# Softmax weights of a small attention copied by DMA instead of spread by matmuls, in a four-stage convolution kernel

## The chip, the cores and the metric

The kernel runs on one core of a Trainium2 chip. Its engines work side by side, each through its own queue of instructions: TensorE (PE; its weight loads are listed as PEld), VectorE (DVE), ScalarE (ACT), GpSimd (POOL) and SyncE (SP), whose queue only starts transfers here. ACT's queue starts transfers too. The transfers themselves run on 16 DMA engines. The metric is device time in microseconds (us), the median of several runs. Less is better.

## The reference

Four convolution-like stages run one after the other on an array x of 8 images, 16 channels and 128 x 128 points, all in float32. The change touches the first: at every point the 3 x 3 neighbourhood is read as three tokens (one for each column) of 48 numbers, which pass through a transformer block with four heads of 12 numbers each.

```
x = fold(in_x)                                # N x 3 tokens x 48, one N for each point
q, k, v = split(layernorm(x) @ w_attn.T, 3)   # each as 4 heads of 12
att = softmax(q . k / sqrt(12))               # 3 x 3 for each point and head
x = x + (att @ v) @ w_attn_proj.T
x = x + gelu(layernorm(x) @ w_fc.T) @ w_fc_proj.T
out = sum over tokens of layernorm(x), through conv_w, + conv_b
```

The other three stages are a gated chain of 1 x 1 convolutions, a convolution of rational functions and a spline convolution. They need what the stage before them wrote.

## The kernel before

**Tiling.** The first stage works on four image rows at a time, a step; there are 32. A tile has two images in its 128 partitions (g = 0 and 1, partitions 64 g and up) and 512 points in its free dimension; so the eight images make four tiles k, which are worked in two halves d, of two tiles each. The tokens of a point are shifted copies of one another along the row: the windows u = 0, 1, 2 of a padded row. So q, k and v are computed once for each point, and the token u of a point takes its neighbours' k and v.

**Steps in flight.** The loop `for n in range(-2, NCH + 3)` (L688 on) holds up to four steps at once: `ahead` (n + 2: its input rows are loaded and centred), `then` (n + 1: layer norm, q, k, v, scores, softmax), `new` (n: attention, projection, first half of the MLP) and `old` (n - 1: rest of the MLP, last norm), and `done` (n - 2: written out). The body issues all their operations in one hand-written order; PE's are tied to it by `in_turn("pe", ...)`, and so are some of DVE's and POOL's. The list `between` holds eight slots: in each, one piece of the attention (`attend`) is followed by pieces of other work.

**Softmax.** `then.softmax` (L510 on) leaves weights in the tile `att`, 96 partitions x 3 x 512: partition 32 u + 8 k + 4 g + h holds the weights of token u, tile k, image g and head h. Its last instruction is the product with the reciprocal of the sum (L529, DVE).

**Attention.** Since the three weights sum to one, a token's result is a middle v plus weighted differences of neighbouring v (`dv`). `attend(k, j, at)` (L533 on) is called eight times a step. It spreads the weights of the heads over the partitions of their numbers with three matmuls against the 0/1 matrix `spread` (into PSUM, `banks`), multiplies them on DVE with the windows of `dv` (L543), and joins the two parts on POOL (L551 and L553). `project(d, u)` (L556 on) multiplies the result with the projection weights on PE and adds the residual on DVE (L565).

**MLP.** `unit(i)` is the MLP for token and half i = 0 to 5: `normed` (a PE product and `h` on DVE, L638), `hidden` (PE and GELU on ACT, `hid`) and `back` (PE, then the residual on DVE, L662). Units 0 to 3 of a step run at the end of its own turn of the loop, units 4 and 5 in the slots of the next.

**PSUM.** PE's results go into eight banks, handed out in pairs by `two()`; while `attend` runs, `ring["from"]` keeps some of them for it.

**Buffers.** Tiles come from pools with a fixed number of buffers; a tile that finds none free waits for the last reader of the oldest. `work` has 11 buffers of 4 KB for each partition, `large` 5 of 6 KB, `xc` 5 of 4 KB. The 0/1 matrices and small constants lie in one tile, `const`, kept through the whole kernel; the weights of the second stage (`w1s`) are loaded at the start of the first.

Of the kernel before, what the change touches and what calls it, by code (L numbers as in the profile page):

```python
# [36 lines left out]
def _constants():  # L37
# [20 lines left out]
    score[token, 24 + 4 * g + h] = 1.0  # L58
    parts["score"] = score
    spread = np.zeros((128, 4, 128))  # L60
    bcast = np.zeros((128, 5, 128))
    last = np.zeros((128, 2, 2, 32))
    for t in range(4):
        bcast[32 * t + 16 + g, 4, token] = 1.0
        for n in range(4):
            bcast[32 * t + 4 * (n // 2) + 2 * (n % 2) + g, n, token] = 1.0
            spread[32 * t + 8 * n + 4 * g + h, n, token] = 1.0
        for u in range(2):
            for k in range(2):
                last[32 * t + 8 + 4 * u + 2 * k + g, u, k, 16 * g + c] = 1.0  # L70
    parts["spread"] = spread.reshape(128, 512)
# [34 lines left out]
def kernel(  # L106
# [29 lines left out]
    from_ = _WHERE["pair"][1]  # L136
    const = cpool.tile([128, _CONST.shape[1] - from_], F32, name="const")
    nc.scalar.dma_start(const, const_in[:, from_:])

    def k_(name):  # L140
        n, lo, hi = _WHERE[name]
        return const[:n, lo - from_ : hi - from_]
# [83 lines left out]
    w1s, b1s = [], []  # L226
    for n in range(5):
        t = cpool.tile([BC, BC], F32, name=f"w1_{n}")
        nc.gpsimd.memset(t, 0.0)
        for b in range(B):  # L230
            r = slice(b * C, (b + 1) * C)
            loads.append((t[r, r], w1[n].rearrange("i o -> o i") if n < 2 else w1[n]))
        w1s.append(t)
        b1s.append(rep(b1[n], B, f"b1_{n}"))
# [7 lines left out]
    with ExitStack() as l0:  # L242
# [19 lines left out]
        def k0(name):  # L262
# [4 lines left out]
        spread, bcast = (  # L267
            k0(name).rearrange("p (n m) -> p n m", m=128) for name in ("spread", "bcast")
        )
# [27 lines left out]
        for i in range(3):  # L297
            for g in range(2):
                r = slice(64 * g + i * 16, 64 * g + i * 16 + 16)
                nc.scalar.dma_start(  # L300
                    wqkv[r, :, :E], w0_qkv[i].rearrange("c (n o) -> c n o", n=3)
                )
                nc.scalar.dma_start(wfc[r], w0_fc[i])
                nc.scalar.dma_start(wcv[r, g * 16 : (g + 1) * 16], w0_conv[i])
# [11 lines left out]
        for g in range(2):  # L316
            nc.scalar.dma_start(wpc[64 * g : 64 * g + E, :E], w0_proj)
# [39 lines left out]
        def work(name):  # L357
            return tmp.tile([128, 2, 512], F32, tag="work", name=name, bufs=11)

        def large(name):  # L360
            return tmp.tile([128, 3, 512], F32, tag="large", name=name, bufs=5)
# [56 lines left out]
        class Step:  # L418
# [23 lines left out]
            def center(self, d):  # L442
                p = two()
                blocks(p, lambda k: wcen[:, 2 * d + k], xin[:, 2 * d : 2 * d + 2])
                self.xc[d] = act.tile([128, 2, 512], F32, name="xc", bufs=5)
# [17 lines left out]
            def qkv(self, d):  # L463
                q = self.q[d] = work("q")
# [19 lines left out]
            def multiply(self, d, engine):  # L484

                for k in range(2):
                    parts = []
                    for at, n in ((0, 3), (3, 2)):
                        t = large("pd")
                        ins = (nc.vector if engine == "dve" else nc.gpsimd).tensor_mul(  # L490
                            t[:, :n].rearrange("p n (a b) -> p n a b", a=4),
# [18 lines left out]
            def softmax(self):  # L510

                a = self.att = act.tile([96, 3, 512], F32, name="att")
                for u in range(3):
                    copy(a[32 * u : 32 * u + 32, 1], banks[32 * u + 32 : 32 * u + 64, 1])
                copy(a[0:64, 2], banks[64:128, 1])
                copy(a[64:96, 2], banks[64:96, 0])
                w = work("mx")
                mx, sm = w[:96, 0], w[:96, 1]
                nc.vector.tensor_max(mx, banks[0:96, 1], a[:, 1])
                nc.vector.tensor_max(mx, mx, a[:, 2])  # L520
                nc.vector.tensor_sub(a[:, 0], banks[0:96, 1], mx)
                for j in (1, 2):
                    nc.gpsimd.tensor_sub(a[:, j], a[:, j], mx)
                yield
                lut(a, a, AF.Exp, scale=1.0 / float(np.sqrt(HD)))
                nc.gpsimd.tensor_add(sm, a[:, 0], a[:, 1])
                nc.gpsimd.tensor_add(sm, sm, a[:, 2])
                nc.vector.reciprocal(sm, sm)
                nc.vector.tensor_mul(  # L529
                    a[:, 0::2], a[:, 0::2], sm.unsqueeze(1).to_broadcast([96, 2, 512])  # L530
                )

            def attend(self, k, j, at):  # L533

                for u in range(3):
                    r = slice(32 * u, 32 * u + 32)
                    pe(banks[:, at + u], spread[r, k], self.att[r, j], start=True, stop=True)
                y = large("y")
                v, dv = (
                    t[k // 2][:, 4 * (k % 2) : 4 * (k % 2) + 4] for t in (self.v, self.dv)  # L540
                )
                out_ = y.rearrange("p n (a b) -> p n a b", a=4)
                ins = nc.vector.tensor_mul(  # L543
                    out_,
                    banks[:, at : at + 3].rearrange("p n (a b) -> p n a b", a=4),
                    windows(dv, j // 2, 3),
                ).ins
                in_turn("dve", ins)
                if j == 0:
                    self.y[k] = y  # L550
                    ins = nc.gpsimd.tensor_sub(out_, windows(v, 1, 3), out_).ins  # L551
                else:
                    ins = nc.gpsimd.tensor_add(self.y[k], self.y[k], y).ins  # L553
                in_turn("pool", ins)

            def project(self, d, u):  # L556
# [3 lines left out]
                for k in range(2):  # L560
                    for r in (0, 64):
                        o = r ^ (64 * k)
                        y = self.y[2 * d + k]
                        pe(p[o : o + 64, k], wpc[r : r + 64], y[r : r + 64, u], start=True, stop=True)
# [29 lines left out]
            def finish(self):  # L594
# [16 lines left out]
                self.rest = work("s")  # L611
                s = self.rest[:, 0]
                nc.gpsimd.tensor_add(rows(s), z[:, 2, :, 0:W], z[:, 1, :, 1 : 1 + W])
                nc.gpsimd.tensor_add(rows(s), rows(s), z[:, 0, :, 2 : 2 + W])

            def store(self):
                cols = bass.ts(self.h0 // 4, 512)
                xl = self.rest[:, 1]
                nc.sync.dma_start(xl, xv[:, cols])
                ins = nc.vector.scalar_tensor_tensor(  # L620
                    xl, self.rest[:, 0], bias0, xl, op0=ALU.add, op1=ALU.add
# [5 lines left out]
                nc.sync.dma_start(x1d[:, cols], xl)  # L627
# [60 lines left out]
        for n in range(-2, NCH + 3):  # L688
# [12 lines left out]
            if old:  # L701
                put(0, old.square, 0)
                u4, u5 = old.unit(4), old.unit(5)
                for i, gen in enumerate((u4, u4, u4, u5, u5, u5)):
                    put(i, next, gen, None)
                put(5, old.vary, 0, 1, var)
# [4 lines left out]
            if new:  # L711
                put(6, new.project, 0, 0)
                put(6, new.project, 0, 1)
                put(7, new.project, 0, 2)
                put(7, new.square, 0)
            if ahead:
                put(7, ahead.center, 0)
            if then:
                put(7, then.scaled, 0)
            if old:  # L720
                put(7, old.vary, 1, 1, var)
            if then:
                put(7, then.qkv, 0)
                put(7, then.scaled, 1)
            if ahead:
                put(7, ahead.center, 1)
            if new:
                put(7, new.vary, 0, 0, var)
            if ahead:
# [5 lines left out]
            ring["from"] = 2 if new else 1  # L735
            for i, fs in enumerate(between):
                if new:

                    new.attend(i // 2, i % 2 * 2, 4 if not old and i < 7 and i % 2 else 1)
                for f in fs:  # L740
                    f()
            ring["from"] = 1
            if new:
                for u in range(3):
                    new.project(1, u)
                new.square(1)
# [4 lines left out]
            if ahead:  # L751
                ahead.first(var)
# [38 lines left out]
    keep = ctx.enter_context(tc.tile_pool(name="keep", bufs=1))  # L791
    for j in range(8):
# [756 lines left out]
```

## Time and profile before

| what | value |
|---|---|
| median of 3 runs | 10417.7 us (10414.69 to 10418.72) |
| the profiled execution | 10417.28 us, span 10415.5 us |
| PE busy in the span | 8808.0 us (85%) |
| DVE busy | 8490.1 us (82%) |
| ACT busy | 8595.5 us (83%) |
| POOL busy | 5545.7 us (53%) |
| first stage | about 50 to 3190 us |
| one step of it, measured in the middle | 94.45 us |
| transfers in the span | 215.74 MB, mean 21 GB/s |

The shares of the whole span mix four stages with different limits. Of the 40 slices in the page's second part, the first twelve are the first stage, and there PE has the digit 9 (6 in the very first) while DVE has 4 to 5, ACT 5 and POOL 6; from the fourteenth slice on, DVE and ACT stand at 9. So for a change in the first stage the whole-span shares of DVE and ACT tell little, and busy times are taken from stretches within the stage. The granted clock of PE is 0.98 to 1.00 in the steps looked at. A matmul of float32 appears as two records in the trace, so 24 matmuls are listed as x48.

### The profile page before, as it was taken

The page shows a single profiled execution, that of the slowest core. Times are in us where ns is not written, and L with a number is a line of the kernel's source. Part 1 is how long each engine was busy: PE and PEld are TensorE (multiplying, and loading weights), DVE is VectorE, ACT ScalarE, POOL GpSimd, SP SyncE. Part 2 cuts the span into 40 slices and gives each one's busy share as a digit, 9 for nine tenths or more (in the row PEclk, how much of TensorE's full clock was granted, in tenths as well). Part 3 has the DMA queues.
Part 4 walks back from the last instruction along what each step waited for, and adds up shares of the span by engine and source line. Part 5 has one row for each costly group of instructions (what it writes and reads, how often), then busy time and mean ns, then how long its engine had stood idle before and what let it go on. Part 6 is the DMA issues. An engine that isn't in the chain of part 4 may idle for free.

```text
span 10415.5 us, 192029 instructions
## 1 busy us (share of the span) xinstructions
PE 8808.0 (85%) x81400; PEld 2482.8 (24%) x81400; DVE 8490.1 (82%) x6774; ACT 8595.5 (83%) x7107; POOL 5545.7 (53%) x2608
## 2 busy tenths in 40 slices
PE   6999999999996888888888888888888888888799
PEld 1222222222222222222222222222222222222222
DVE  4545554554555999999999999999999999999977
ACT  3555555555555999999999999999999999999988
POOL 4666666666652555555555555555555555555421
PEclk8999999999998999999999999999999999999999
DMA  1000000000002000000000000000000000000022
GB/s 53 13 15 15 14 14 15 15 13 15 15 7 77 14 21 16 18 21 14 21 14 21 14 20 21 14 21 14 21 14 21 17 18 20 14 13 9 14 62 62
DMA packets 203668, 215.74 MB, mean 21 GB/s; under 512 B 50616, under 2 KB 159416, under 8 KB 200760
## 3 DMA queue, kind: packets, MB, share of 16 engines
q1 hardware_dynamic: 197544, 198.27, 7.0%
q8 instruction: 640, 10.49, 0.4%
q10 hardware_dynamic: 5264, 5.17, 0.2%
q14 instruction: 220, 1.80, 0.1%
HBM read 117.80 MB, written 60.04 MB: 17 GB/s over the span
## 4 chain that ended last, share of the span: by engine, by line
DVE 43%; PE 25%; issue 21%; ACT 8%; DMA 2%; SPq 1%; POOL 0%; DVEq 0%; ACTq 0%; POOLq 0%
PE banks L375 18%; DVE u L1078 15%; DVE pn L1078 10%; DVE u L1082 9%; DVE t L1068 2%; PE pn L1019 2%; PE pd L1019 2%; PE acc L1398 2%; DVE y L543 2%; DVE x L565 1%; ACT hid L157 1%; ACT sq L571 1%; ACT u L157 1%; DMA f<-yd 1%; DVE x L662 1%
## 5 line engine op out<-in xcount | busy, mean ns | idle before, releaser
L1091 POOL TENSOR_TENSOR v<-t,u 128x1280 f32<-128x1280 f32 x1152 | 3449.8, 2995 | 3080.8 <-DVE t L1068 3044.7
L1068 DVE SCALAR_TENSOR_TENSOR t<-t,u 128x2048 f32<-128x2048 f32 x1152 | 2632.7, 2285 | 32.3 <-ACT u L157 31.2
L1019 PE MATMUL pd<-f,wb 32*64 32x512 f32 x18432 | 2510.2, 608 | 92.8 <-ACT t L1057 40.5
L1057 ACT ACTIVATE t<-pd 128x1024 f32<-128x1024 f32 x2304 | 2364.9, 1026 | 133.2 <-PE pd L1019 75.0
L1019 PE MATMUL pn<-f,wa 32*64 32x512 f32 x18432 | 1299.4, 615 | 1112.1 <-DVE u L1082 1111.9
L157 ACT ACTIVATE u<-u 128x2048 f32<-128x2048 f32 x1152 | 2208.9, 1917 | 0.0
L157 ACT ACTIVATE u<-t 128x2048 f32<-128x2048 f32 x1152 | 2204.0, 1913 | 0.0
L1078 DVE TENSOR_TENSOR u<-pn,u 128x1280 f32<-128x1280 f32 x1152 | 1718.8, 1492 | 122.2 <-DVE pn L1078 2.8
L157 ACT ACTIVATE hid<-banks 128x1024 f32<-128x1024 f32 x576 | 569.9, 1023 | 1049.6 <-PE banks L375 1048.3
L1110 PE MATMUL acc<-u,const 128*32 128x512 f32 (+2 forms) x13824 | 1112.1, 454 | 0.0
L1078 DVE TENSOR_TENSOR pn<-pn,u 128x768 f32<-128x768 f32 x1152 | 1103.3, 958 | 0.0
L1082 DVE SCALAR_TENSOR_TENSOR u<-t,pn 128x768 f32<-128x768 f32 x1152 | 1087.6, 944 | 0.0
L1019 PEld LDWEIGHTS pd<-f,wb 32*64 32x64 f32 x18432 | 615.1, 130 | 1249.6 <-ACT t L1057 891.8
L1019 PEld LDWEIGHTS pn<-f,wa 32*64 32x64 f32 x18432 | 275.7, 130 | 2117.2 <-DVE u L1082 2109.7
L1110 PE MATMUL acc<-v,const 128*32 128x512 f32 (+1 forms) x9216 | 763.2, 449 | 1.5 <-POOL v L1091 1.5
L490 POOL TENSOR_TENSOR pd<-q,kp 128x1536 f32<-128x1536 f32 x248 | 674.6, 2732 | 11.2 <-PE banks L375 9.1
L571 ACT ACTIVATE sq<-x 128x1024 f32<-128x1024 f32 x384 | 395.3, 1053 | 272.6 <-DVE x L565 172.8
L375 PE MATMUL banks<-h,wfc 64*128 64x512 f32 (+1 forms) x3072 | 598.5, 617 | 14.6 <-DVE h L638 14.6
L638 DVE TENSOR_TENSOR h<-banks,x 128x1024 f32<-128x1024 f32 x192 | 232.6, 1211 | 428.2 <-PE banks L375 219.2
L543 DVE TENSOR_TENSOR y<-banks,dv 128x1536 f32<-128x1536 f32 x256 | 448.2, 1751 | 140.4 <-PE banks L375 134.1
L1110 PEld LDWEIGHTS acc<-u,const 128*32 128x32 f32 x13824 | 366.6, 109 | 812.6 <-issue 812.6
L553 POOL TENSOR_TENSOR y<-y 128x1536 f32<-128x1536 f32 x128 | 442.1, 3454 | 197.8 <-DVE y L543 197.5
(198 smaller groups left out, 8370.6 us busy)
## 6 DMA issues: line engine op xcount, KB each, us to landing
f<-yd SPq DMA_DIRECT2D x1016, 60.9 KB
yd<-y SPq DMA_DIRECT2D x280, 130.0 KB
xin<-in_x SPq DMA_DIRECT2D x744, 32.0 KB
four<-sil SPq DMA_DIRECT2D x256, 65.0 KB
xj<-in_x SPq DMA_DIRECT2D x8, 1024.0 KB
s<-in_x SPq DMA_DIRECT2D x32, 256.0 KB
x1d<-s SPq DMA_DIRECT2D x32, 256.0 KB
x<-x1d SPq DMA_DIRECT2D x8, 1024.0 KB
```

What stands on the lines that cost most here:

```text
L157: ins = nc.scalar.activation(out_, in_, func, **kw).ins
L375: in_turn("pe", mm(*args, skip_group_check=True, **kw).ins)
L490: ins = (nc.vector if engine == "dve" else nc.gpsimd).tensor_mul(t[:, :n].rearrange("p n (a b) -> p n a b", a=4), rows(self.q[d][:, k]).un ...
L543: ins = nc.vector.tensor_mul(out_, banks[:, at : at + 3].rearrange("p n (a b) -> p n a b", a=4), windows(dv, j // 2, 3),).ins
L571: nc.scalar.activation(self.sq[d][u], self.x2[d][:, u], AF.Square)
L1019: yield mm(p[64 * (u % 2) : 64 * (u % 2) + 64, u // 2], w[lo : lo + 32, q % 2, n].rearrange("p c f -> p (c f)"), fs[k * NP + q][lo : lo + ...
L1057: in_turn("act", nc.scalar.activation(self.t[:, ab], self.pd, AF.Abs).ins)
L1068: ins = nc.vector.scalar_tensor_tensor(self.t, self.t, 1.0, self.u, op0=ALU.add, op1=ALU.mult).ins
L1078: in_turn("dve", nc.vector.tensor_mul(u if cols.start else p, p, u).ins)
L1082: ins = nc.vector.scalar_tensor_tensor(u, t, 2.0, p, op0=ALU.subtract, op1=ALU.mult).ins
L1091: ins = nc.gpsimd.tensor_mul(self.v, t, u).ins
L1110: ins = mm(accs[k][32 * q : 32 * q + 32, lo % 512 : (hi - 1) % 512 + 1], gather[:, int(part == 1), g], flat(c.u)[:, ab, lo:hi] if src is N ...
```

## The change

In words:

- `attend` no longer uses PE. It is called for half d and token u, six times a step, and for each of the half's two tiles starts a transfer on SP's queue that reads the 8 partitions of `att` that belong to token u and tile k, each row of 1024 numbers (left and right weight) 16 times, and writes 128 partitions of a tile `y`. DVE multiplies `y` in place with two windows of `dv` and subtracts one half from the other; POOL adds the token's own v.
- For this the heads lie 16 partitions apart instead of 12: `wqkv`, `wpc` and `score` are laid out anew, `wqkv` by 18 loads instead of 6, `wpc` by 8 instead of 2. `spread` is gone. The softmax's planes are ordered left, right, middle.
- `project` of all six (d, u) runs in the slots, two slots behind its `attend`; before, the first half ran in slots 6 and 7 and the second after the slots. `center` and `scaled` move from slot 7 to slot 6, `square(0)` of the old step from slot 0 to slot 2, `square(1)` of the new one and `ahead.first` into slot 7. `ring["from"]` is 1 throughout.
- `store` works in the space of `z`, and its transfer to DRAM is started by `write`, in slot 7.
- Buffers: `work` 9 instead of 11, `xc` 4 instead of 5, `q`, `pd` and `y` with buffers of their own (`q` 2 of 4 KB, `pd` 2 of 6 KB and 3 of 4 KB, `y` 4 of 4 KB) instead of `work` and `large`.
- Most constants and the weights `w1s` are loaded between the first and the second stage, on ACT's queue; `w1s` were loaded on SP's queue in the first stage.

```diff
-    score[token, 24 + 4 * g + h] = 1.0
+    score[64 * g + 16 * h + r % HD, 24 + 4 * g + h] = 1.0
...
-    w1s, b1s = [], []
-    for n in range(5):
-        t = cpool.tile([BC, BC], F32, name=f"w1_{n}")
-        nc.gpsimd.memset(t, 0.0)
-        for b in range(B):
-            r = slice(b * C, (b + 1) * C)
-            loads.append((t[r, r], w1[n].rearrange("i o -> o i") if n < 2 else w1[n]))
-        w1s.append(t)
-        b1s.append(rep(b1[n], B, f"b1_{n}"))
+    b1s = [rep(b1[n], B, f"b1_{n}") for n in range(5)]
...
-                nc.scalar.dma_start(
-                    wqkv[r, :, :E], w0_qkv[i].rearrange("c (n o) -> c n o", n=3)
-                )
+                for n in range(3):
+                    nc.scalar.dma_start(
+                        wqkv[r, n].rearrange("c (h d) -> c h d", h=NH)[:, :, :HD],
+                        w0_qkv[i][:, n * E : (n + 1) * E].rearrange("c (h d) -> c h d", h=NH),
+                    )
...
-            nc.scalar.dma_start(wpc[64 * g : 64 * g + E, :E], w0_proj)
+            for h in range(NH):
+                lo = 64 * g + 16 * h
+                nc.scalar.dma_start(wpc[lo : lo + HD, :E], w0_proj[h * HD : (h + 1) * HD])
...
         def work(name):
-            return tmp.tile([128, 2, 512], F32, tag="work", name=name, bufs=11)
-
-        def large(name):
-            return tmp.tile([128, 3, 512], F32, tag="large", name=name, bufs=5)
+            return tmp.tile([128, 2, 512], F32, tag="work", name=name, bufs=9)
...
-                self.xc[d] = act.tile([128, 2, 512], F32, name="xc", bufs=5)
+                self.xc[d] = act.tile([128, 2, 512], F32, name="xc", bufs=4)
...
-                q = self.q[d] = work("q")
+                q = self.q[d] = tmp.tile([128, 2, 512], F32, name="q", bufs=2)
...
-                        t = large("pd")
+                        t = tmp.tile([128, n, 512], F32, name=f"pd{n}", bufs=5 - n)
...
-            def attend(self, k, j, at):
-
-                for u in range(3):
-                    r = slice(32 * u, 32 * u + 32)
-                    pe(banks[:, at + u], spread[r, k], self.att[r, j], start=True, stop=True)
-                y = large("y")
-                v, dv = (
-                    t[k // 2][:, 4 * (k % 2) : 4 * (k % 2) + 4] for t in (self.v, self.dv)
-                )
-                out_ = y.rearrange("p n (a b) -> p n a b", a=4)
-                ins = nc.vector.tensor_mul(
-                    out_,
-                    banks[:, at : at + 3].rearrange("p n (a b) -> p n a b", a=4),
-                    windows(dv, j // 2, 3),
-                ).ins
-                in_turn("dve", ins)
-                if j == 0:
-                    self.y[k] = y
-                    ins = nc.gpsimd.tensor_sub(out_, windows(v, 1, 3), out_).ins
-                else:
-                    ins = nc.gpsimd.tensor_add(self.y[k], self.y[k], y).ins
-                in_turn("pool", ins)
+            def attend(self, d, u):
+
+                for k in (2 * d, 2 * d + 1):
+                    y = tmp.tile([128, 2, 512], F32, name="y", bufs=4)
+                    lo = 32 * u + 8 * k
+                    nc.sync.dma_start(
+                        y.rearrange("p n m -> p (n m)"),
+                        self.att[lo : lo + 8, 0:2]
+                        .rearrange("h n m -> h (n m)")
+                        .unsqueeze(1)
+                        .to_broadcast([8, 16, 1024]),
+                    )
+                    v, dv = (t[d][:, 4 * (k % 2) : 4 * (k % 2) + 4] for t in (self.v, self.dv))
+                    out_ = y.rearrange("p n (a b) -> p n a b", a=4)
+                    in_turn("dve", nc.vector.tensor_mul(out_, out_, windows(dv, u, 2)).ins)
+                    in_turn("dve", nc.vector.tensor_sub(y[:, 0], y[:, 1], y[:, 0]).ins)
+                    at = rows(y[:, 0])
+                    ins = nc.gpsimd.tensor_add(at, at, v[:, :, u + 1 : u + 1 + W]).ins
+                    in_turn("pool", ins)
+                    self.y[k, u] = y
...
             def store(self):
                 cols = bass.ts(self.h0 // 4, 512)
-                xl = self.rest[:, 1]
+                xl = self.z.rearrange("p n a b -> p (n a b)")[:, :512]
                 nc.sync.dma_start(xl, xv[:, cols])
...
-                nc.sync.dma_start(x1d[:, cols], xl)
+                self.last = x1d[:, cols], xl
+
+            def write(self):
+                nc.sync.dma_start(*self.last)
...
-            ring["from"] = 2 if new else 1
             for i, fs in enumerate(between):
-                if new:
-
-                    new.attend(i // 2, i % 2 * 2, 4 if not old and i < 7 and i % 2 else 1)
+                if new and i > 1:
+                    new.project(*divmod(i - 2, 3))
+                if new and i < 6:
+                    new.attend(*divmod(i, 3))
                 for f in fs:
                     f()
-            ring["from"] = 1
-            if new:
-                for u in range(3):
-                    new.project(1, u)
-                new.square(1)
...
+    constants(keep, "const", _WHERE["pair"][2], _CONST.shape[1])
...
+        w1s = []
+        for n in range(5):
+            t = wp.tile([BC, BC], F32, name=f"w1_{n}")
+            nc.gpsimd.memset(t, 0.0)
+            for b in range(B):
+                r = slice(b * C, (b + 1) * C)
+                nc.scalar.dma_start(t[r, r], w1[n].rearrange("i o -> o i") if n < 2 else w1[n])
+            w1s.append(t)
```

## The prediction

> **What bounds the kernel now.** I read the page first, then busy time by stretch, then the timeline of one step, then the rates of single transfers. The change lies in the first stage, some 50 to 3190 us, which runs 32 steps. The windows view cuts out one step (1499.48 to the same matmul group of the next at 1593.93) and its two parts:
>
> ```profile
> core 0: us, PE busy (x) PEld busy (x) DVE busy (x) ACT busy (x) POOL busy (x), PEclk, DMA share, GB/s
> 1499.48:1593.93 94.45, 85.64 (x532) 23.73 (x528) 49.06 (x41) 52.42 (x56) 60.66 (x35) 1.00 0.06 14
> 1547.20:1583.55 36.35, 32.76 (x193) 9.12 (x193) 26.27 (x20) 17.12 (x17) 26.57 (x8) 1.00 0.05 14
> 1583.55:1641.65 58.10, 54.57 (x338) 14.90 (x336) 22.79 (x21) 33.60 (x37) 34.07 (x26) 0.97 0.06 15
> ```
>
> PE is busy 85.64 of 94.45 us; no other engine reaches two thirds, and the DMA engines are nearly unused (0.06). PE works in a fixed order, so what PE does or waits for is the step. The first part runs from the moment the softmax weights are ready (end of DVE L529) to the first qkv product; the change lies there. In its timeline the spreading products stand between those of the MLP:
>
> ```profile
> 1547.25 1.14 PE L375 MATMUL banks<-att,const 32*128 32x512 f32 x6 [2.13 <-DVE att L529]
> 1548.32 1.99 PE L375 MATMUL banks<-h,wfc 64*128 64x512 f32 x8
> ...
> 1558.53 1.13 PE L375 MATMUL banks<-att,const 32*128 32x512 f32 x6 [1.00 <-DVE y L543]
> ```
>
> A group of six holds PE 1.07 us (start to start), eight groups a step, and the brackets are waits for them. The costs of the other engines come from the groups of instructions in the stage, by form:
>
> ```profile
> L543 DVE TENSOR_TENSOR y<-banks,dv 128x1536 f32<-128x1536 f32 x256 | 448.2, 1751 | 140.4 <-PE banks L375 134.1 <-POOL y L553 5.4
> L529 DVE TENSOR_TENSOR att<-att,mx 96x1024 f32<-96x1024 f32 x32 | 38.7, 1208 | 0.1
> L520 DVE TENSOR_TENSOR mx<-mx,att 96x512 f32<-96x512 f32 x32 | 22.0, 688 | 3.3
> L613 POOL TENSOR_TENSOR s<-z 128x512 f32<-128x512 f32 x32 | 35.0, 1093 | 0.2
> L909 DVE TENSOR_SCALAR y<-x,mean,rs 128x1024 f32<-128x1024 f32 x16 | 12.8, 799 | 0.0
> ```
>
> **Removed.** On PE, 8 x 1.07 = 8.6 us a step and the waits bound to them in this part (2.13 + 1.6 = 3.7). On DVE, 8 x 1.75 = 14.0; on POOL, 4 x 3.19 + 4 x 3.45 = 26.6 us. PE alone would then need 36.35 - 8.6 = 27.8 us for this part, plus the second half's projections, which move into it (2.8 us, taken out of the second part): 30.6. The second part shrinks to 58.10 - 2.8 = 55.3.
>
> **Added on DVE and POOL.** Twelve times a step a 1024-wide product of two SBUF tensors (L529: 1.21) and a 512-wide difference (L520: 0.69): 22.8 us of DVE; on POOL 12 x 1.09 = 13.1. In the built order these DVE instructions stand in one queue with h (1.2), two x2 updates of the MLP (2.4), five of the six projection sums (6.1) and the store's three (2.1), all before the last projection can run: 34.6 us. Each product waits for its copy, and h, which PE needs, queues behind.
>
> **Added on the DMA queue.** Twelve copies a step, each from 8 partitions (4 KB rows, every row 16 times) to 128, 524,288 bytes. No row shows that shape, so I bound it. Four transfers of this trace, each cut to its middle so that start and end don't count: from 16 partitions (o<-x), from 32 (four<-sil), from 128 (yd<-y), and a 128-row load over 3.4 us (xj):
>
> ```profile
> 9874.50:9874.65 0.15, 0.00 (x0) 0.00 (x0) 0.15 (x1) 0.15 (x1) 0.00 (x0) 0.50 0.56 99
> 9870.00:9870.20 0.20, 0.20 (x4) 0.04 (x1) 0.06 (x1) 0.20 (x2) 0.00 (x0) 0.50 0.81 179
> 5796.05:5796.30 0.25, 0.25 (x8) 0.16 (x8) 0.25 (x1) 0.25 (x1) 0.00 (x0) 1.00 1.02 358
> 20.92:24.32 3.40, 0.00 (x0) 0.00 (x0) 1.52 (x3) 0.00 (x0) 0.00 (x0) 1.00 0.98 322
> ```
>
> The last number is GB/s. It falls with the partitions read: 358, 179, 99, that is some 6 GB/s for each source partition once they are few. Fast end: the wide rate, 524,288 / 322,000 = 1.6 us. Slow end: 32-partition rate by four, 45 GB/s, 11.7 us. The nearest row is the 16-partition one, SBUF to SBUF on the same queue: 99 / 2 = 49.5 GB/s, 10.6 us; its engines were only 0.56 busy, still starting, so I round down to 10.0 us. Twelve take 120 us and follow each other: four y buffers keep at least one copy queued, since a landed pair is used up (1.9 + 1.9 on DVE, 1.1 POOL, 0.5 PE) while the next pair runs. The Trainium skill (SBUF — State Buffer, "Door 1: The DMA port swizzle") ties the rate to the ports that the partitions reach, 27.2 GB/s for four neighbours; 8 partitions are two ports, 54 GB/s, an estimate of 9.6 us a copy and about 13,100 us in the sum below. DMA: Bandwidth & Descriptors ("Why a DMA increments its semaphore by 16 and not by 1") adds that the slowest dimension sets the number of engines, here 8 of 16. Both speak against the change; no run here shows either for this shape.
>
> **The sum.** The first part becomes the longest of PE 30.6, DVE (below) and the copies: 1.2 us to the first packet (0.9 from issue to first data in a load f<-yd, plus semaphores), 120, then the last pair's DVE 1.9, POOL 1.1, PE 0.5 and the variance products 1.9 ahead of qkv: 126.6. Step: 126.6 + 55.3 = 181.9 against 94.45, +87.5; 32 steps +2,800 us. PE's saved 12.3 us vanish in the wait. Late next: qkv, the scores, the following softmax, so nothing of the next step covers it.
>
> **Edges.** ACT's queue starts 18 more weight loads (0.57 us each, 10), of which the 5.9 us that its Sqrt waited for DVE covers half: +5. Between the stages the 40 loads of w1 now stand on ACT before its Sqrt, where before only bs stood: 40 x 0.48 (what SP took for them) + the constants and their wait: +21. Together +26.
>
> **At no cost:** the padded head layout (same matmul shapes); pd, q and the nine work tiles and four xc tiles (xc's oldest is read by a sum that ends before the copy that reuses it is evacuated; otherwise 1.0 us of ACT is late); the store in z's space and its later write (nobody waits until the stage ends); center and scaled one place ahead, behind which nothing new queues. The input loads on SP wait for PE's center products at the step's end anyway, after the last copy was issued.
>
> The profiled run spans 10,415.5 (10,417.28 with its ends), the runs' median is 10,417.7; I add to that: 10,417.7 + 2,800 + 26 = **13,245 us**. With copies of 9.0 to 11.7 us (32 x 12 = 384 of them): 12,860 to 13,900.
>
> **Rivals.**
> 1. The copies run at the wide rate and DVE becomes the bound. Then 2.8 us to the first landing, 34.6 of DVE, 1.1 + 0.5 + 1.9: 40.9, step 96.2, +56 +26: 10,500. If DVE and POOL hinder each other on SBUF operands (the products of L490 on DVE took 1211 to 2958 ns at the start, beside POOL work), up to 13.1 more: 10,920. For it: 16 engines are idle. Against: the three rates above. Middle 10,700.
> 2. The copy is held at what 16 partitions gave, 99 GB/s, whatever its source: 5.3 us, 63.6 a step, step 125.5: +994 +26, 11,440. For it: each engine writes several rows; against: the rate doubled from 16 to 32.
> 3. Faster: copies at the wide rate, and the two DVE instructions at L909's 0.78 ns an element instead of L529's 1.18: 12 x (0.80 + 0.40) = 14.4 instead of 22.8, DVE 26.2, part 32.5, step 87.8, -213 +26: 10,230. It decides when landing, DVE and tail stay under 38.3 us (94.45 - 55.3 - 26/32). Against: L529 has just this pair of operands, and so has L520.
> 4. It doesn't do what it says: between 1 and 3 the saving and the new waits cancel, 10,418.
>
> **Chances.** Forecast 0.58, rival 1 0.15, rival 2 0.12, rival 3 0.12, rival 4 0.03. Beside 0.2% (21 us, about what a measurement tells from no change): faster 0.12, within 0.03, slower 0.85. The predicted time is the forecast's; its own range is 12,860 to 13,900. To leave out no more than 2 in 10 the range goes down into rival 1: 10,600 to 13,600 (out: rivals 3 and 4, the low end of 1, the top of the forecast).
>
> **What would show it.** Right: steps near 180 us; y's copies 10 us apart, q1's share low in engines yet never idle; DVE y waiting for DMA and PE for POOL y; PE's share near 45% in the stage. Rival 1: steps under 110 us, DVE without gaps after the first landing. Wrong at the root: copies landing under 3 us apart, or steps under 94 us. The edges: ACT's Sqrt between the stages some 21 us later after the last step.

## The result, and the profile after

| kernel | median of 4 runs | range | profiled execution: span |
|---|---|---|---|
| before | 10416.19 us | 10413.32 to 10418.72 | 10415.5 us |
| changed | 12234.61 us | 12224.12 to 12235.55 | 12233.8 us |

The changed kernel takes 1.1744 times as long (95% interval 1.1723 to 1.1764), 1,818 us more. The forecast was 13,245 us.

The page of the changed kernel, parts 1 and 2 (busy time; busy tenths and granted PE clock in 40 slices):

```profile
PE 8969.4 (73%) x79864; PEld 2468.8 (20%) x79864; DVE 8749.6 (72%) x7286; ACT 8577.6 (70%) x7107; POOL 5159.7 (42%) x2736
...
PE   4666666666666666688888888888888888888899
...
PEclk7777777777777777799999999999999999999999
```

Busy times hardly moved; the span grew. In the first sixteen slices, the first stage, no engine is busy more than six tenths, where PE had stood at 9. The windows of one step, split as in the prediction at the first qkv product:

```profile
core 0: us, PE busy (x) PEld busy (x) DVE busy (x) ACT busy (x) POOL busy (x), PEclk, DMA share, GB/s
2066.40:2163.40 97.00, 43.88 (x172) 9.64 (x168) 37.92 (x39) 16.20 (x17) 14.09 (x12) 0.67 0.40 71
2163.40:2218.10 54.70, 50.46 (x318) 14.13 (x316) 19.32 (x18) 36.08 (x40) 34.13 (x26) 1.00 0.06 15
```

The first part grew from 36.35 to 97.00 us, the second shrank from 58.10 to 54.70. The groups of instructions say who waits for whom (behind the bar: busy us, mean ns, then idle time before it and its releaser):

```profile
L542 DVE TENSOR_TENSOR y<-y,dv 128x1024 f32<-128x1024 f32 x384 | 472.0, 1229 | 1856.6 <-DMA y<-att 1856.5
L369 PE MATMUL banks<-y,wpc 64*64 64x512 f32 x1536 | 550.6, 908 | 1500.6 <-POOL y L545 1467.5
L545 POOL TENSOR_TENSOR y<-y,vp 128x512 f32<-128x512 f32 x384 | 450.6, 1173 | 2660.4 <-DVE y L543 2639.5
```

DVE waits 1,857 us for the copies, about as much as the 1,818 us that the kernel lost; POOL waits for DVE, and PE for POOL. In DVE's timeline of that step the first copy and the last two look like this (the weights are ready at 2066.4):

```profile
2065.18 1.21 DVE L524 TENSOR_TENSOR att<-att,mx 96x1024 f32<-96x1024 f32 x1
2066.31 1.21 DVE L657 TENSOR_TENSOR x<-banks,x 128x1024 f32<-128x1024 f32 x1
2078.59 1.23 DVE L542 TENSOR_TENSOR y<-y,dv 128x1024 f32<-128x1024 f32 x1 [11.07 <-DMA y<-att]
...
2151.50 1.23 DVE L542 TENSOR_TENSOR y<-y,dv 128x1024 f32<-128x1024 f32 x1 [2.08 <-DMA y<-att]
2152.76 0.69 DVE L543 TENSOR_TENSOR y<-y 128x512 f32<-128x512 f32 x1
2155.98 1.23 DVE L542 TENSOR_TENSOR y<-y,dv 128x1024 f32<-128x1024 f32 x1 [2.53 <-DMA y<-att]
```

So 97.0 = 12.2 to the first landing + 77.4 for eleven more copies, 7.04 us each in the mean + 7.4 from the last landing to the qkv products. The eleven distances are uneven, 4.28 to 9.86 us, in much the same order from step to step; the copies of token 2, which read partitions 64 and up, follow their predecessor soonest (4.3 to 5.0 us). The step shown ends with two of these.

**Where the 1,818 us are.** The last softmax instruction (L529, after: L524) starts 32 times, from 105.6 to 3080.8 us before and from 103.3 to 4801.3 after. A step therefore takes 95.97 us in the mean before and 151.55 after: 31 x 55.6 = 1,723. The transition to the second stage (last z product to the first gate) takes 33.7 us more, the start 2.3 less; the last step and what drains behind it make up the rest.

The transition, in the timeline of the changed kernel:

```profile
4973.96 32.88 ACTq L802 DMA_DIRECT2D w<-in_w  x40
...
5007.70 14.13 ACTq L846 DMA_DIRECT2D bs<-in_w_base  x8
...
5021.86 1.28 ACT L160 ACT_TABLE_LOAD   x1 [50.41 <-DMA dense<-in_a]
5023.16 0.20 ACT L160 ACTIVATE s<-var 128x1 f32<-128x1 f32 x1
```

Starting these loads takes up ACT's queue for 47 us. The Sqrt that everything waits for (last line) had its input at 4989.67 and starts 33 us later.

### The profile page after: what moved, and what is told of

The parts are those of the page before. It is cut to its first block, busy times and chain, and to the rows that moved or that the text cites. A ratio compares the mean times of both kernels' runs of the same rounds, so it can differ in the third digit from the quotient of the medians.

```text
span 12233.8 us, 190898 instructions
## 1 busy us (share of the span) xinstructions
PE 8969.4 (73%) x79864; PEld 2468.8 (20%) x79864; DVE 8749.6 (72%) x7286; ACT 8577.6 (70%) x7107; POOL 5159.7 (42%) x2736
## 4 chain that ended last, share of the span: by engine, by line
DVE 36%; DMA 20%; issue 19%; PE 17%; ACT 4%; SPq 2%; POOL 1%; DVEq 0%; ACTq 0%; POOLq 0%
DMA y<-att 18%; DVE u L1079 13%; PE banks L369 12%; DVE pn L1079 9%; DVE u L1083 8%; DVE t L1069 2%; PE pn L1020 1%; PE acc L1399 1%; SPq L533 1%; PE pd L1020 1%; DVE y L542 1%; POOL y L545 1%; DMA f<-yd 1%; ACT att L366 1%; ACT hid L160 1%
## 5 line engine op out<-in xcount | busy, mean ns | idle before, releaser
L1058 ACT ACTIVATE t<-pd 128x1024 f32<-128x1024 f32 x2304 | 2360.3, 1024 | 129.7 <-PE pd L1020 66.7
L542 DVE TENSOR_TENSOR y<-y,dv 128x1024 f32<-128x1024 f32 x384 | 472.0, 1229 | 1856.6 <-DMA y<-att 1856.5
L369 PE MATMUL banks<-y,wpc 64*64 64x512 f32 x1536 | 550.6, 908 | 1500.6 <-POOL y L545 1467.5
L545 POOL TENSOR_TENSOR y<-y,vp 128x512 f32<-128x512 f32 x384 | 450.6, 1173 | 2660.4 <-DVE y L543 2639.5
L369 PE MATMUL banks<-h,wfc 64*128 64x512 f32 (+1 forms) x3072 | 750.7, 719 | 267.8 <-DVE h L633 236.9
```

The lines of the kernel that those rows point to most:

```text
L369: in_turn("pe", mm(*args, skip_group_check=True, **kw).ins)
L542: in_turn("dve", nc.vector.tensor_mul(out_, out_, windows(dv, u, 2)).ins)
L545: ins = nc.gpsimd.tensor_add(at, at, v[:, :, u + 1 : u + 1 + W]).ins
L1058: in_turn("act", nc.scalar.activation(self.t[:, ab], self.pd, AF.Abs).ins)
```

## The experiments

All times are medians, one execution unless a range is given; the kernel before took 10,418 to 10,421 us beside them. "Step" is the mean distance of the last softmax instruction over 31 steps, "copy" the mean distance of two landings or, where DVE is the bound, of two starts that no buffer holds up.

| run | what is different | us | step | copy |
|---|---|---|---|---|
| before | | 10,418 | 95.97 | |
| changed | | 12,234.6 | 151.55 | 7.04 |
| e1 | copies all read the same 8 partitions | 13,522.9 | 191.9 | 10.57 |
| e5 | every second copy on ACT's queue | 12,113.4 | 147.8 | |
| e3 | copies read from DRAM | 11,192.2 | 118.9 | 4.4 |
| e9 | from DRAM, outermost dimension 16 | 10,788.3 | 106.5 | 2.2 |
| e2 | from 128 partitions, no repetition | 10,675.9 | 102.95 | |
| e10 | e2, half the differences on POOL | 10,663.4 | 102.4 | |
| e11 | e9, half the differences on POOL | 10,873.3 | 109.2 | |
| e12 | e2 without the differences | 10,306.3 | 91.3 | |
| e13 | e2 without POOL's additions | 10,403.4 | 94.6 | |
| e4 | spread by PE again, rest as changed | 10,884.7 | 109.7 | |
| e6 | e4, spreading in pairs of row groups | 10,793.0 | 106.7 | |
| e7 | e6, w1 loaded early again | 10,756.6 | 106.2 | |

### What bounds a copy: e1, e2, e3, e9, e5

e1, for every tile the same weights:

```diff
-                    lo = 32 * u + 8 * k
+                    lo = 0
```

> Every copy reads the same 8 partitions of the weights instead of those of its token and tile (so the attention uses wrong weights). In the changed kernel a copy's packets take 618 ns against 156 ns for the fastest, and the copies come 6.6 us apart. Theory (the source's few partitions hold a copy to some 50 GB/s, and copies that follow each other gain only because they read other partitions and so overlap): no overlap is left, copies 9.9 us apart, step 12.2 + 11 x 9.9 + 11.9 + 54.7 = 188 us, in all about 13,400 us. Rival (the 6.6 us come from the engines or the write side, whatever is read): no change, 12,230 us.

Measured: 13,522.9 us. DVE's timeline shows the landings:

```profile
3196.45 1.23 DVE L542 TENSOR_TENSOR y<-y,dv 128x1024 f32<-128x1024 f32 x1 [8.64 <-DMA y<-att]
3197.71 0.69 DVE L543 TENSOR_TENSOR y<-y 128x512 f32<-128x512 f32 x1
3206.92 1.23 DVE L542 TENSOR_TENSOR y<-y,dv 128x1024 f32<-128x1024 f32 x1 [8.52 <-DMA y<-att]
...
3217.46 1.23 DVE L542 TENSOR_TENSOR y<-y,dv 128x1024 f32<-128x1024 f32 x1 [7.58 <-DMA y<-att]
```

They are 10.5 us apart, 10.57 in the mean of the step: 49.6 GB/s. In the trace's packet records a packet of 4 KB takes 619 ns (median) and mostly 7 or 8 are under way at once. In the changed kernel, where two copies in a row read different groups of 8 partitions, nearly all packets take 156 to 638 ns (median 314) and the mean distance falls to 7.04 us (the expectation put it at 6.6). Nothing but the partitions read differs, so copies that read the same partitions hinder each other, and copies that read others overlap on one queue.

e2 takes the narrow source away. It gives `att` 128 partitions (the last 32 set to zero) and leaves out the repetition of each head's weights, so `y` holds other numbers. With that the outermost dimension of the copy rises from 8 to 128 too, so e2 alone doesn't tell the two apart:

```diff
-                        self.att[lo : lo + 8, 0:2]
-                        .rearrange("h n m -> h (n m)")
-                        .unsqueeze(1)
-                        .to_broadcast([8, 16, 1024]),
+                        self.att[:, 0:2].rearrange("p n m -> p (n m)"),
```

> The same 512 KB are copied, but row by row from all 128 partitions of a weights tile made 128 high (32 rows of zeros), so nothing is repeated and the attention uses wrong weights. Theory (the source's partitions are the limit): 1.5 to 2.5 us a copy, DVE and PE set the step again, 96 to 104 us, in all 10,450 to 10,750. Rival (bytes written, or latency and the four y buffers, are the limit): still over 11,500.

Measured: 10,675.9 us. Same bytes, same queue, but 159 ns a packet and 16 at a time; DVE waits for copies 62.7 us in all (group of L541, shown below with e10), not 1,857.

e3 keeps the repetition and reads it from DRAM instead, written there once a step:

```diff
+                self.attd = dram.tile([96, 1024], F32, name="attd", bufs=2)
+                nc.sync.dma_start(self.attd, a[:, 0:2].rearrange("p n m -> p (n m)"))
...
-                        self.att[lo : lo + 8, 0:2]
-                        .rearrange("h n m -> h (n m)")
+                        self.attd[lo : lo + 8]
```

> The weights go to DRAM once a step (384 KB) and the twelve copies read them from there, each row 16 times. Theory (the SBUF source is the limit): with 8 engines at 156 ns a packet 2.5 us a copy, up to 4.8 if the written partitions hold it back; 3 us more before the first copy; step 100 to 122, in all 10,600 to 11,300. Rival (the repetition of rows or the few engines are the limit): as in the changed kernel or more, 12,200.

Measured: 11,192.2 us, within the theory's range; 258 ns a packet, still mostly 8 at a time, a copy every 4.4 us, and the first lands 10 us after the softmax. So at 8 engines the SBUF source costs as well: 7.04 us against 4.4. Whether a copy from 8 SBUF partitions gains from 16 engines wasn't tried. e9 writes every row twice, so that the copy's outermost dimension is 16:

```diff
-                self.attd = dram.tile([96, 1024], F32, name="attd", bufs=2)
+                self.attd = dram.tile([96, 2, 1024], F32, name="attd", bufs=2)
...
                         self.attd[lo : lo + 8]
+                        .rearrange("h c m -> (h c) m")
                         .unsqueeze(1)
-                        .to_broadcast([8, 16, 1024]),
+                        .to_broadcast([16, 8, 1024]),
```

> e3 with every row of weights written twice to DRAM, so that the outermost dimension of a copy is 16 and not 8. In e3 exactly 8 packets are under way at a time, 258 ns each, and a copy takes 4.4 us. Theory (a copy with an outermost dimension of 8 uses 8 DMA engines, and that is what bounds e3): 16 packets at a time, 2.1 to 2.6 us a copy, VectorE's work in the first part of the step becomes the bound, step 108 to 113 us, 10,840 to 11,000 us. Rival (the reads of one row or the writes of y are the bound, or packets take twice as long): 11,150 to 11,300 us.

Measured: 10,788.3 us, below the range of the theory: the mechanism was right, its effect undersized. Mostly 16 or 17 packets are under way while the copies run, and two copies that no buffer holds up start 2.2 us apart. The Trainium skill (DMA: Bandwidth & Descriptors, "Why a DMA increments its semaphore by 16 and not by 1") says that the slowest dimension of the access patterns sets the number of DMA engines; e3 with 8 packets at a time and e9 with 16 agree. The windows of one step's first part show the same, e3 first, then e9:

```profile
2247.30:2305.80 58.50, 35.13 (x126) 7.92 (x124) 31.66 (x35) 12.83 (x13) 12.81 (x11) 0.72 0.49 119
```

```profile
2018.95:2071.00 52.05, 36.11 (x178) 8.89 (x180) 41.45 (x39) 16.51 (x17) 21.67 (x12) 0.87 0.58 147
```

With 8 engines the DMA share (next to last) stands just under one half, which looks like room and is the limit. In e9 the copies wait for DVE instead: it is busy 41.45 of 52.05 us, the rest being the way through DRAM.

e5 puts every second copy on ACT's queue:

```diff
-                    nc.sync.dma_start(
+                    (nc.scalar if k % 2 else nc.sync).dma_start(
```

> The changed kernel with every second copy on ScalarE's queue. Consecutive copies read different groups of 8 partitions. Theory (each copy is bound by the read side of its own 8 partitions; two at a time fill the engines better): a copy takes 5 to 6 us in the mean instead of 7.0, 11,400 to 11,900 us. Rival (a second queue adds nothing to the same engines, and ScalarE waits at its copies for free buffers): 12,110 us or more.

Measured: 12,113.4 us, at the border of the rival and 1% below the changed kernel. In one step (154.4 us, longer than the run's mean of 147.8) 8 packets are under way together at most, but for 1.5 of 90 us, as on one queue, and a packet takes 418 ns in the mean instead of 381. The first two copies land together 23 us after the softmax instead of the first after 12. The second queue adds no engine; that agrees with the page just named ("Issuing engines are not separate DMA queues").

### What the change costs without the copies: e4, e6, e7, e10 to e13

e4 keeps order, buffers and head layout, but spreads by PE again (two matmuls a tile into PSUM; product into a tile `both`, difference into `y`):

```diff
-                    nc.sync.dma_start(
-                        y.rearrange("p n m -> p (n m)"),
...
+                    p, r = two(), slice(32 * u, 32 * u + 32)
+                    for j in range(2):
+                        pe(p[:, j], spread[r, k], self.att[r, j], start=True, stop=True)
```

> The changed kernel with the spreading done by PE again (four matmuls for each half and token, 24 a step as before), all else of the change kept: order, padded heads, two-window products, buffers (y of 2 KB and one product tile instead of y of 4 KB). Theory (the copies are all of the loss but the edges): step 93 to 98 us, in all 10,380 to 10,580. Rival (the new order and the longer DVE work cost much by themselves): step over 105, in all over 10,750.

Measured (median of 4 runs): 10,884.7 us (10,871.1 to 10,891.1), ratio 1.0448 (1.0431 to 1.0466). The theory fell, and the rival's figures came (step 109.7), though in part for another cause. The windows of the first part, before, then e4:

```profile
2122.99:2160.45 37.46, 33.44 (x193) 9.38 (x193) 26.26 (x20) 18.56 (x19) 26.57 (x8) 1.00 0.04 14
```

```profile
2191.79:2249.47 57.68, 57.57 (x216) 17.74 (x216) 39.09 (x40) 15.52 (x16) 14.21 (x12) 0.82 0.03 9
```

Two things grew. PE is now busy without a gap; its spreading products take 794.1 us in the stage instead of 342.4, because e4 puts four in a row on the same 32 rows of the array (3.7 us), where the kernel before put three on three groups of rows (1.1 us). The rows of the spreading, before, e4, then e6 (below):

```profile
L375 PE MATMUL banks<-att,const 32*128 32x512 f32 x1536 | 342.4, 658 | 93.0 <-DVE y L543 49.0 <-DVE att L529 44.0
```

```profile
L374 PE MATMUL banks<-att,const 32*128 32x512 f32 x1536 | 794.1, 662 | 77.9 <-DVE att L529 77.7
```

```profile
L374 PE MATMUL banks<-att,const 32*128 32x512 f32 x1536 | 552.5, 709 | 87.9 <-DVE att L529 61.4 <-DVE y L547 26.0
```

The longer spreading belongs to e4's form, not to the change. And DVE has 39.1 us of work there instead of 26.3: the change gives it the differences, which POOL had, and the projections' sums.

e6 takes most of the first cause away by issuing two tiles of different row groups in turn. It changes two things besides: the product is done by two instructions, one of which leaves its result in PSUM, and the projection follows a slot later:

```diff
-                    p, r = two(), slice(32 * u, 32 * u + 32)
-                    for j in range(2):
-                        pe(p[:, j], spread[r, k], self.att[r, j], start=True, stop=True)
+                ps = [two() for _ in pair]
+                for j in range(2):
+                    for p, (k, u) in zip(ps, pair):
+                        r = slice(32 * u, 32 * u + 32)
+                        pe(p[:, j], spread[r, k], self.att[r, j], start=True, stop=True)
```

> The kernel e4 again, but the spreading matmuls of two tiles that read different groups of 32 rows of the weights are issued alternately (in e4 all four of a pair read the same 32 rows), the products stay in PSUM, and a projection follows one slot later. In e4 the spreading takes 3.7 us for four matmuls, 22 us a step, against 1.13 us for three on three groups of rows, 9 us a step, in the kernel before. Theory (the 466 us that e4 lost are mostly these matmuls standing one behind the other, not the new order): about 2 us for a pair, 12 us a step, so 10 us a step less than e4: 10,480 to 10,640 us. Rival (the order of the work, VectorE's chain or the late projections cost it): within 100 us of e4, 10,790 us or more.

Measured (median of 4 runs): 10,793.0 us (10,782.1 to 10,797.0), ratio 1.0359 (1.0344 to 1.0374). The theory fell; the rival's bound of 10,790 is met by 3 us, less than the runs spread. The spreading fell to 552.5 us, 7.5 us a step less, but the step fell by 3.0 only. In e7, which has the same order, PE then waits in that part:

```profile
2116.42:2169.74 53.32, 48.43 (x216) 13.77 (x217) 39.27 (x51) 18.52 (x19) 14.30 (x12) 0.87 0.05 13
```

PE is busy 48.43 of 53.32 us at a clock of 0.87; most of the gaps end with a difference on DVE. So 3.0 of e4's 13.7 us a step went with its row groups, and the rest stays. How much of the rest is DVE's work, the new order or the lower clock, these runs do not separate.

e7 is e6 with the removed lines that load `w1s` in the first stage put back.

> e6 with the weights of the next stage loaded at the start of the kernel again, as in the kernel before. Theory (ScalarE's queue issues these 27 or more loads between the stages, and the Sqrt stands behind them, +34 us): 25 to 36 us less than e6. Rival (the loads of x set the start of the next stage anyway): less than 8 us of difference.

Measured (median of 4 runs): 10,756.6 us (10,753.3 to 10,760.8), 36.5 us less than e6. In the profiled executions 12 us of the difference lie in the steps and 30 in the time behind the last softmax, as the theory said.

e10 goes on from e2, whose DVE works without a gap from the first landing to the last product, and in all 40.49 of the first part's 48.40 us:

```profile
2159.10:2207.50 48.40, 34.52 (x170) 8.41 (x166) 40.49 (x39) 16.03 (x17) 21.89 (x13) 0.93 0.35 141
```

It moves every second difference to POOL:

```diff
-                    in_turn("dve", nc.vector.tensor_sub(y[:, 0], y[:, 1], y[:, 0]).ins)
+                    if k % 2:
+                        in_turn("pool", nc.gpsimd.tensor_sub(y[:, 0], y[:, 1], y[:, 0]).ins)
+                    else:
+                        in_turn("dve", nc.vector.tensor_sub(y[:, 0], y[:, 1], y[:, 0]).ins)
```

> e2 (copies from 128 partitions without repetition) with the difference of every second tile on GpSimd instead of VectorE. Theory (what is left of the change once the copies cost little is VectorE's work in the first part of the step, 39.3 us against 26.3 us in the kernel before, which it does there without a gap): six differences of 0.69 to 1.47 us leave VectorE, 4 to 9 us a step, 10,390 to 10,550 us against e2's 10,676. Rival (GpSimd, whose adds already take 1.7 us there instead of 1.1, becomes the bound, or the projections' chain is): 10,640 us or more. Like e2 it leaves out the repetition of each head's weights, so the values of y are not those of the reference.

Measured: 10,663.4 us, 0.1% under e2, which single executions cannot tell from no gain; the rival. The groups of e2, then of e10:

```profile
L544 POOL TENSOR_TENSOR y<-y,vp 128x512 f32<-128x512 f32 x384 | 656.7, 1713 | 739.8 <-DVE y L542 725.0 <-PE banks L369 12.3
L541 DVE TENSOR_TENSOR y<-y,dv 128x1024 f32<-128x1024 f32 x384 | 498.5, 1298 | 62.7 <-DMA y<-att 62.7
L542 DVE TENSOR_TENSOR y<-y 128x512 f32<-128x512 f32 x384 | 345.8, 900 | 5.6
```

```profile
L541 DVE TENSOR_TENSOR y<-y,dv 128x1024 f32<-128x1024 f32 x384 | 609.1, 1593 | 62.9 <-DMA y<-att 62.6
L543 POOL TENSOR_TENSOR y<-y 128x512 f32<-128x512 f32 x192 | 290.0, 1510 | 36.3 <-DVE y L541 36.3
L545 DVE TENSOR_TENSOR y<-y 128x512 f32<-128x512 f32 x192 | 188.3, 981 | 3.4
```

DVE lost 345.8 - 188.3 = 157.5 us of differences and got 609.1 - 498.5 = 110.6 us of longer products. e11 does the same to e9:

> e9 (weights through DRAM, copies with an outermost dimension of 16) with the difference of every second tile on GpSimd instead of VectorE. Theory as for e10: 4 to 9 us a step less than e9's 106.5 us, 10,500 to 10,660 us; about 10 us a step of waiting for the way through DRAM stay. Rival: 10,750 us or more.

Measured: 10,873.3 us, the rival, even 85 us slower than e9; its products on DVE take 1,569 ns instead of 1,376, while the differences left on DVE fall from 883 to 715.

e12 and e13 take work out of e2 instead of moving it: e12 the line with the difference on DVE, e13 the addition of v on POOL.

> e2 without the twelve differences of a step on VectorE (left out: the subtraction of the two weighted neighbours; GpSimd adds v to the first alone). Theory (with cheap copies VectorE's work in the first part is the bound): 12 x 0.90 = 10.8 us of VectorE leave a part that it fills, 7 to 10 us a step, 10,350 to 10,450 us against e2's 10,676. Rival (something else, the order of the projections or TensorE, holds that part): 10,600 us or more.

Measured: 10,306.3 us, 11.7 us a step less than e2, for 10.8 us of DVE taken out; the theory, with a larger gain than its range. The addition on POOL takes 1,438 instead of 1,713 ns there, which may be part of it; the product on DVE, in turn, rose from 1,298 to 1,469.

> e2 without the twelve additions of v on GpSimd (left out: v itself). Theory (VectorE's instructions with two operands in SBUF and GpSimd's slow each other: differences 0.90 us in e2 against 0.69, products 1.30 against 1.22): both go back to 0.69 and 1.22 us, 12 x 0.29 = 3.5 us a step, and 1.7 us at the end of the last tile: 3 to 6 us a step, 10,480 to 10,580 us. Rival (the slow differences have another cause, the layout or the copies that arrive meanwhile): they keep 0.85 us or more and the time stays above 10,600 us.

Measured: 10,403.4 us, 8.4 us a step less, more than the theory's range. Its groups:

```profile
L541 DVE TENSOR_TENSOR y<-y,dv 128x1024 f32<-128x1024 f32 x384 | 467.9, 1219 | 63.1 <-DMA y<-att 63.0
L542 DVE TENSOR_TENSOR y<-y 128x512 f32<-128x512 f32 x384 | 263.2, 686 | 5.5
```

The difference is back at 686 ns and the product at 1,219, as L520 and L529 had it: 12 x (900 - 686 + 1298 - 1219) = 3.5 us of the 8.4. That the rest is the addition itself, which stood between DVE and every projection, is an inference.

None of the versions tried that computes everything is faster than the kernel before. The nearest, e7 and e9, stay 3 to 4% behind. Adding v by PE in the projection instead of by POOL, on top of e9, wasn't tried.

## Why the prediction was right in sign and 8% too high

- **Sign and range.** Copies bound the step, as forecast: DVE y waits for DMA, PE for POOL y. But 12,234.6 us lie below the forecast's own 12,860 to 13,900 and above rival 2's 11,440; no rival gives them. That they lie within 10,600 to 13,600 is owed to the width of that range, which was stretched down for rival 1; it is luck. Of the signs named, copies 10 us apart and steps near 180 us did not come (7.04 and 151.6).
- **The step that failed** is "Twelve take 120 us and follow each other". Copies that follow each other do take about what the nearest row said: 10.57 us in e1 against the 10.0 taken. That the row served is partly luck, since the four transfers differ in more than the partitions read: the packets of the 16-partition one are 512 bytes long, those of the others 520, 1040 and 8192, and the copies' are 4096. But neighbours in this kernel read different partitions and overlap: eleven distances were 77.4 us, not 110, 32.6 a step, 1,043 over 32. That is the miss of 1,010, but for small terms that nearly cancel. The price was taken from single transfers; what two neighbouring copies share was not asked. (The base step, cut out at 94.45, was also 1.5 us shorter than the mean, 95.97.)
- **The other terms of the first part** held: first landing 12.2 us after the softmax (1.2 + 10.0 = 11.2 forecast), tail 7.4 (5.4; a projection's sum of 1.1 us stood between product and difference, the rest lies in POOL's addition, 1.27, and the projection, 1.3). The second part was 54.7 us (55.3).
- **Edges:** -2.3 at the start (forecast +5), +33.7 at the transition (+21): the 40 loads of w1 took ACT's queue 32.88 us, 0.82 each, not the 0.48 that SP had taken. Starting one took ACT 0.44 us in the mean, no more than SP; the rest is pauses between them, whose cause is open. e7 shows that these loads are what delays the stage. Sum 31 against 26.
- **"At no cost"** held for the buffers as far as the changed kernel shows: its second part is as short as forecast. For the new order it is open: e4, e6 and e7, without the copies, still take 10 to 14 us a step more than the kernel before.
- **PE's share** was to be near 45% in the stage; in the step shown it is (43.88 + 50.46) / 151.7 = 62%. The step is shorter than forecast, and PE, which does not do more, has instructions that last longer: its granted clock is 0.67 in the first part, and a projection's matmul takes 908 ns in the mean instead of 606.
- **Rival 1** did not happen, but its place is real: e2, with cheap copies, is DVE-bound at 10,676 (middle of the rival: 10,700), and the hindrance between DVE and POOL that it priced at up to 13.1 us is what e13 shows, with 3.5 us of DVE's time a step.
- **Rival 2** (99 GB/s whatever the source) was wrong in its cause: the source decides, from 49.6 GB/s (e1) over 74 (524,288 bytes in 7.04 us) to 119 (e3, 4.4 us).
- **Rival 3** needed the products at L909's rate; they took 1,229 ns, like L529. **Rival 4** needed a step that stays; none did.

So of the 55.6 us a step, 48.6 go away with cheap copies (151.55 - 102.95 in e2); the other 7.0 hang on DVE's longer work in the first part and on the additions beside it: e12 and e13 each gain more than 7.0 by taking one of them out. How they share the 7.0 was not separated.

## What to carry to other kernels

In these runs a copy that fans a few SBUF partitions out to 128 was priced by the partitions that it reads and by its outermost dimension, not by the bytes alone: the same 524,288 bytes took from 10.57 us down to 2.2. If it must be done, going through DRAM with an outermost dimension of 16 let copies follow 2.2 us apart here where SBUF as a source took 7.04, but the first one landed only 9 to 10 us after the softmax. Before pricing twelve copies as twelve times one, look at whether neighbours read the same partitions. Work taken off the busiest engine helps only if what replaces it does not land on the next one: here PE was relieved of 8.6 us and DVE given 13 in the same part of the step.

## What the runs showed of the hardware that was not expected

- **Copies on one queue overlap.** With 8 engines, packets of 4 KB took 619 ns when all copies read the same 8 partitions, and 314 (median) when neighbouring copies read others. What lets them overlap was not shown.
- **DVE and POOL slow each other when DVE reads two SBUF operands.** Difference and product take 686 and 1,219 ns in the mean without POOL's additions (e13), 900 and 1,298 with them (e2), 981 and 1,593 in e10; POOL's addition takes 1,173 ns in the changed kernel, where they seldom meet, and 1,713 in e2. The means mix two cases: in e2's trace 102 of the 384 differences overlap an addition and take 1,508 ns, the other 282 take 681. The Trainium skill (SBUF — State Buffer, "Who interferes with whom") states this for DVE instructions with two inputs in SBUF beside a GpSimd instruction that reads SBUF, and not for those with one; e4 agrees: its products read PSUM, 177 of 384 overlap an addition, and they take 1,225 ns against 1,222 for the others.

```profile
L543 DVE TENSOR_TENSOR both<-banks,dv 128x1024 f32<-128x1024 f32 x384 | 469.8, 1224 | 148.5 <-PE banks L374 128.4 <-DVE y L544 0.9
L546 POOL TENSOR_TENSOR y<-y,vp 128x512 f32<-128x512 f32 x384 | 454.3, 1183 | 1163.3 <-DVE y L544 1159.5 <-PE banks L374 3.8
```

- **PE's granted clock fell where PE waited.** It is 0.67 in the changed first part against 1.00 before, 0.61 in e1's, 0.93 in e2's (48.40 us). The projection's matmul took 908 ns in the mean; before it took 606:

```profile
L375 PE MATMUL banks<-y,wpc 64*64 64x512 f32 x1536 | 196.4, 606 | 19.2 <-DVE x L662 15.1 <-ACT sq L448 2.8 <-POOL y L553 1.3
```

Waiting is not all of it: in e4's first part PE is listed as busy 57.57 of 57.68 us, at 0.82. What sets the clock was not tested, nor how much of the 97 us it costs.
